# Graph network kernel: each step of finishing a block follows the step it needs by a group of sums, and the ring of gather places keeps its size up to the layers' ends

## The chip, the cores and the metric

The kernel runs on one core of one Trainium2 chip. The time is the device time of one execution in microseconds (us); smaller is better. The five engines named here are TensorE (PE; its weight loads are listed apart as PEld), VectorE (DVE), ScalarE (ACT), GpSimd (POOL) and SyncE (SP). Each works through its own list of instructions in order, and they wait for each other by semaphores. POOL and SP also issue DMA transfers.

## The reference

A graph with N = 6250 nodes of D = 512 features and E = 100000 edges, sorted by their destination. All is float32. The part that matters:

```python
h = relu(layernorm(x))
norm = -dinv[src] * dinv[dst]            # dinv = 1/sqrt(number of edges that leave a node)

def conv(h, W0, W1, b):
    gathered = segment_sum(h[src] * norm[:, None], dst, num_segments=N)
    return h @ W0 + gathered @ W1 + b

h = conv(h, W1_0, W1_1, b1)
h = leaky_relu(layernorm(h) * gamma + beta, 0.01)
return x + conv(h, W2_0, W2_1, b2)
```

So there are two layers, and each of them needs, for every node, the sum over its incoming edges of the rows of the source nodes, one product of that sum with a 512 x 512 matrix, and one product of the node's own row with another.

## The kernel before

**Edges, chunks and groups.** The edges are laid out in 782 chunks of at most 128 edges. Three chunks (STEP) belong to one window of 32 destination nodes, and four windows make a group, so a group has 12 chunks; there are 66 groups (NS) in a layer, of which the first has one window. The main loop runs over the layers and, in each, over the groups g.

**Gathers.** For each chunk POOL issues one indirect DMA (`gather_to`, L548), which fetches the 128 source rows of the chunk from a table in HBM into one of the numbered places of an array in SBUF (`places`). The function `ring` gives each chunk its place, and with it `prev`, the chunk that had that place before. At group g, `gather_to` issues every chunk whose place was last held by a chunk of a group that is already written into the program as summed; on the chip, POOL then waits for the sums of that earlier chunk. The ring has a size of 63 places in its first round and 55 in the next ones, and then shrinks round by round, to 35 (WIDE) in layer 0 and to 26 (NARROW) in layer 1.

**Sums.** DVE builds a one-hot matrix `sel` of edges against the 32 nodes of a window (`choose`, L689, from node numbers prepared by L678), one group ahead. In layer 0 DVE also multiplies it by the scale of the source rows, which came with the gathered rows (`scale`, L729). PE multiplies each of the group's 12 chunks with its part of `sel` into `ps` (`sums`, L745; 24 matmuls in the trace). ACT copies the result to SBUF as `agg` (L760). `sel` has three buffers, `ps` two, `agg` three.

**Finishing a block.** The nodes are also cut into 49 blocks of 128. Windows of 32 nodes drift against them, so a block takes its rows from two or three groups. For a block there are these steps on PE, with the others between:

1. *placing* (`place`, L781): PE multiplies the `agg` of the block's groups with one-hot matrices `there` (DVE, L768) into `an_ps`; ACT scales that to `an` (L880).
2. *transposes* (`first_half`, L888): four transposes of `an` into `hT_ps`; DVE copies them to `aT` (L890; one buffer).
3. *own products* (`own_products`, L648): the block's own rows, which SP loaded and DVE transposed to `hT` (L632), times the first matrix, into `u_ps` (two buffers).
4. *second products* (`second`, L643): `aT` times the second matrix, added into the same `u_ps`.
5. *finish*: in layer 0 DVE adds the bias and normalizes (L849 to L859), ACT and DVE apply the leaky relu (L862, L863), and SP stores the rows as the table of layer 1; in layer 1 DVE adds bias and x (L843, L844) and SP stores the output.

Three blocks are finished in four groups. `turn` does the loads, the DVE transposition of the own rows and the placing of one block; `second` of the block before is written in it ahead of the placing.

**What sets the order.** The lists of PE, POOL and SP are exactly in the order in which the program is written (`manual_schedule`). DVE and ACT are put in order by a scheduler, which follows the program with some freedom; `issue_after` forces single instructions behind others (so `scale` behind the last `there`, `aT` and the like, held in `behind`). In one pass of the group loop the program writes: the gathers; placing of the blocks that became complete, with the `second` of the block before; `sel` and `scale`; the group's sums; and then the transposes and own products of the blocks just placed. In groups 3 to 5 of layer 0 (SOON) the sums come first. From group 54 on (JOIN) a block's `second` follows its `first_half` directly (`dense`), and four of the last blocks (EARLY) have their own products made in advance.

## Time and profile before

| | |
|---|---|
| median of 3 runs | 2356.39 us (2353.88 to 2360.64) |
| the profiled execution | 2366.06 us |
| its span (first to last instruction) | 2364.3 us |
| mean granted clock of PE | 0.845 |
| PE matmuls busy | 1715.6 us (73% of the span) |
| POOL busy | 1490.9 us (63%) |
| DVE busy | 741.3 us (31%) |
| ACT busy | 332.3 us (14%) |

The profile is of one execution, whose span starts with the first instruction. A row of the timeline gives the start, the duration, the engine and line, what the instruction writes and reads with its shapes, how many equal instructions were drawn together (x), and in brackets how long the engine had been idle before and what ended that. The view of waits gives for an engine and line what it waited for, the total in us, how many times, and the longest. "issue" means a wait for nothing that the profile shows, "remote" that the releaser could not be named. The end of a PE matmul is modelled, so a PE row may end later in truth than the row says. The main loop of layer 0 fills the span to about 1250 us, that of layer 1 the rest.

### The profile page before, as it was taken

The page shows a single profiled execution, that of the slowest core. Times are in us where ns is not written, and L with a number is a line of the kernel's source. Part 1 is how long each engine was busy: PE and PEld are TensorE (multiplying, and loading weights), DVE is VectorE, ACT ScalarE, POOL GpSimd, SP SyncE. Part 2 cuts the span into 40 slices and gives each one's busy share as a digit, 9 for nine tenths or more (in the row PEclk, how much of TensorE's full clock was granted, in tenths as well). Part 3 has the DMA queues.
Part 4 walks back from the last instruction along what each step waited for, and adds up shares of the span by engine and source line. Part 5 has one row for each costly group of instructions (what it writes and reads, how often), then busy time and mean ns, then how long its engine had stood idle before and what let it go on. Part 6 is the DMA issues. An engine that isn't in the chain of part 4 may idle for free.

```text
span 2364.3 us, 18838 instructions
## 1 busy us (share of the span) xinstructions
PE 1715.6 (73%) x6458; PEld 663.8 (28%) x6458; DVE 741.3 (31%) x1554; ACT 332.3 (14%) x605; POOL 1490.9 (63%) x1578
## 2 busy tenths in 40 slices
PE   5377876676788767777757577787767787676777
PEld 4233322222233222222222222222222222222223
DVE  8754433323334334332323112221112122112221
ACT  8564110101011110110100000000000000000000
POOL 4545566666676666666645666666666666666663
PEclk9668987888888888888877788887888888888888
DMA  9976777777787767777756777777777776777773
GB/s 352 348 239 194 202 217 209 214 214 209 214 238 205 209 198 219 217 219 206 227 151 178 209 231 222 215 216 216 215 223 213 227 219 202 223 231 223 228 214 117
DMA packets 225517, 515.56 MB, mean 218 GB/s; under 512 B 38795, under 2 KB 90569, under 8 KB 225413
## 3 DMA queue, kind: packets, MB, share of 16 engines
q0 software_dynamic: 125120, 415.88, 59.9%
q1 hardware_dynamic: 100253, 98.38, 13.2%
q8 instruction: 53, 0.87, 0.2%
q14 instruction: 51, 0.42, 0.1%
q10 hardware_dynamic: 40, 0.02, 0.0%
HBM read 475.25 MB, written 38.86 MB: 217 GB/s over the span
## 4 chain that ended last, share of the span: by engine, by line
PE 40%; another core or an unknown queue 25%; issue 15%; POOL 9%; DVE 6%; DMA 2%; ACT 2%; SPq 0%; DVEq 0%; ACTq 0%; POOLq 0%
PE u_ps L643 12%; PE ps L745 9%; POOL places L548 9%; PE u_ps L648 9%; PE an_ps L781 6%; PE hT_ps L888 2%; DMA places<-tab,sidx 1%; DVE hi L417 1%; DVE aT L890 1%; DVE lo L417 1%; ACT agg L760 1%; DVE sel L689 1%; DVE there L768 1%; PE hT_ps L598 1%
## 5 line engine op out<-in xcount | busy, mean ns | idle before, releaser
L548 POOL DMA_INDIRECT places<-tab,sidx x1191 | 1133.1, 951 | 604.6 <-issue 332.9
L745 PE MATMUL ps<-places,sel 128*32 128x512 f32 x3104 | 461.2, 656 | 56.9 <-issue 50.8
L781 PE MATMUL an_ps<-agg,there 128*128 128x512 f32 (+1 forms) x554 | 281.1, 635 | 109.7 <-ACT agg L760 65.0
L548 POOL DMA_INDIRECT places<-tab,lidx x270 | 256.2, 949 | 129.2 <-issue 74.1
L643 PE MATMUL u_ps<-places,aT 128*128 128x512 f32 x384 | 226.0, 742 | 140.4 <-DVE aT L890 136.6
L689 DVE TENSOR_TENSOR sel<-dlx,nodes_ps 128x384 f32<-128x384 f32 (+3 forms) x134 | 72.4, 541 | 723.3 <-remote 518.9
L643 PE MATMUL u_ps<-w,aT 128*128 128x512 f32 x384 | 208.1, 692 | 83.2 <-DVE aT L890 71.0
L745 PEld LDWEIGHTS ps<-places,sel 128*32 128x32 f32 x3104 | 101.3, 117 | 391.3 <-issue 367.1
L760 ACT ACTIVATE agg<-ps 128x512 f32<-128x512 f32 (+2 forms) x130 | 76.4, 590 | 938.5 <-remote 667.1
L648 PE MATMUL u_ps<-w,hT 128*128 128x512 f32 x392 | 198.5, 647 | 9.7 <-issue 9.6
L648 PE MATMUL u_ps<-places,hT 128*128 128x512 f32 x392 | 189.9, 625 | 9.8 <-issue 9.7
L781 PEld LDWEIGHTS an_ps<-agg,there 128*128 128x128 f32 (+1 forms) x554 | 104.1, 197 | 261.0 <-issue 183.6
L643 PEld LDWEIGHTS u_ps<-places,aT 128*128 128x128 f32 x384 | 88.7, 241 | 276.5 <-DVE aT L890 165.7
L888 PE MATMUL hT_ps<-ident,an 128*128 128x128 f32 x384 | 69.8, 309 | 117.5 <-ACT an L880 67.5
L643 PEld LDWEIGHTS u_ps<-w,aT 128*128 128x128 f32 x384 | 82.8, 222 | 204.5 <-issue 115.6
L768 DVE TENSOR_SCALAR there<-iota_r,node_of 128x128 f32<-128x128 f32 (+1 forms) x286 | 66.9, 294 | 154.1 <-remote 71.6
L632 DVE STREAM_TRANSPOSE hT<-h 128x512 f32<-128x512 f32 x90 | 63.5, 705 | 139.5 <-PE u_ps L648 44.9
L648 PEld LDWEIGHTS u_ps<-w,hT 128*128 128x128 f32 x392 | 78.2, 210 | 96.9 <-issue 96.1
L888 PEld LDWEIGHTS hT_ps<-ident,an 128*128 128x128 f32 x384 | 44.6, 152 | 206.2 <-issue 120.6
L648 PEld LDWEIGHTS u_ps<-places,hT 128*128 128x128 f32 x392 | 75.2, 202 | 89.3 <-issue 89.3
L843 DVE SCALAR_TENSOR_TENSOR u_ps<-u_ps,root,bias 128x512 f32<-128x512 f32 x45 | 34.1, 759 | 202.5 <-PE u_ps L643 105.2
L849 DVE TENSOR_TENSOR u_ps<-u_ps,bias 128x512 f32<-128x512 f32 x45 | 31.5, 699 | 183.4 <-PE u_ps L643 66.0
(196 smaller groups left out, 1139.2 us busy)
## 6 DMA issues: line engine op xcount, KB each, us to landing
h<-tab SPq DMA_DIRECT2D x360, 64.0 KB
places<-tab,sidx POOLq DMA_INDIRECT x1191
xt<-in_x_dram SPq DMA_DIRECT2D x48, 256.0 KB
out_dram<-t SPq DMA_DIRECT2D x48, 256.0 KB
tab<-t SPq DMA_DIRECT2D x46, 256.0 KB
tab<-places SPq DMA_DIRECT2D x22, 528.0 KB
places<-in_x_dram SPq DMA_DIRECT2D x5, 1792.0 KB
places<-tab,lidx POOLq DMA_INDIRECT x270
```

What stands on the lines that cost most here:

```text
L417: made = nc.vector.tensor_tensor(t, s[:, g * 2 * GJ : (g + 1) * 2 * GJ].rearrange("p (j s) -> p j s", s=2)[:, :, None, :] .to_broadcast([E ...
L548: nc.gpsimd.indirect_dma_start(out=places[:, slot(t), :] if own_scale else zr(layer, t), out_offset=None, in_=x if layer == 0 and t < RAW ...
L632: nc.vector.transpose(hT.rearrange("p k (a i) -> p k a i", i=Q), own_h.pop(i).rearrange("p (a k d) -> p k a d", a=NQ, d=Q))
L643: nc.tensor.matmul(u_ps[:r], hT[:, kc, :r], w[:, kc, :], start=(start and kc == 0), stop=(stop and kc == KD - 1))
L648: nc.tensor.matmul(u_ps, hT[:, kc, :], w[:, kc, :], start=(kc == 0), stop=(stop and kc == KD - 1))
L689: nc.vector.tensor_tensor(sel[:, q : q + k, :w, :], of, node[:, q : q + k, None, :].to_broadcast([P, k, w, Q]), op=OP.is_equal)
L745: members.append(nc.tensor.matmul(to, sel[:, q, s, :], rows_of, start=(s == 0), stop=(s == len(chunk[q]) - 1 and (cnt is None or chunk[q][ ...
L760: nc.scalar.activation(agg[g][: n * Q, lo : lo + w], ps[: n * Q, lo : lo + w], AF.Copy)
L768: behind[1] = nc.vector.tensor_scalar(t[:m, :r], iota_r[:m, :r], node_of[:m, g : g + 1], -(1.0 + i * P), op0=OP.subtract, op1=OP.is_equal)
L781: all_of.append(nc.tensor.matmul(placed[i][:r], t[:m, :r], agg[g][:m, :], start=(g == inside[i][0]), stop=(g == inside[i][-1])))
L843: nc.vector.scalar_tensor_tensor(v, v, root[:r, i : i + 1], bias2[:r], op0=OP.mult, op1=OP.add)
L888: nc.tensor.transpose(ps[:, kc, :r], an[:r, kc * P : (kc + 1) * P], ident[:r, :r])
```

## The change

In groups 0 to 47 of both layers (`deep`; DEEP = 18 groups are left then) the steps are written in another order. A pass of the loop now holds: the gathers, `sel` of the next group and (layer 0) `scale` of the next group; the sums of the group; `second` of the block whose transposes were written in an earlier pass; the transposes and own products of the blocks placed in an earlier pass; and then the placing of the blocks that are complete now. At group 48 what is outstanding is written out at once. From group 48 to 53 the placing stands ahead of the sums, as before, and `second` of the block before comes behind the sums instead of ahead of the placing; from group 54 on only the ring is different. The special case of groups 3 to 5 is gone. The extra buffers for `agg` (`wide`, every other group, in buffers named `pre`) are used up to group 47 in both layers instead of up to group 7 of layer 0. The ring keeps 55 places until 165 chunks or fewer are left in a layer, and then shrinks by 8 (DROP) a round to 35 or 26; in layer 1 it goes back to 55 first. The numbers of instructions are the same but for two fewer on DVE.

The diff:

```diff
@@ -38,6 +38,8 @@
 SPREAD = 16
 WIDE = 35
 NARROW = 26
+DROP = 8
+DEEP = 18
 
 
 def parts(r):
@@ -54,10 +56,9 @@
             prev.append(last.get(k, -1))
             last[k] = len(slots)
             slots.append(k)
-        if size == most:
-            size = full
-        elif len(slots) > most + 2 * full:
-            size -= 2 if size > WIDE else 3 if size > NARROW and len(slots) > chunks + full else 0
+        layer, at = divmod(len(slots), chunks)
+        left = chunks - at
+        size = full if left > 3 * full else max(WIDE if layer == 0 else NARROW, size - DROP)
     return slots[: 2 * chunks], prev[: 2 * chunks]
 
 
@@ -497,7 +498,6 @@
                           "minus unsorted dinv sdinv bias1 bias2 gam bet unseen unit N E D NB NC NU NS KD rows places "
                           "R load_rest sc pick quads src_hi zero_row p_id lent X src W").split())
     AHEAD = 2
-    SOON = range(3, 6)
     EARLY = {NB - 4: NS - 13, NB - 3: NS - 11, NB - 2: NS - 9, NB - 1: NS - 7}
     ACT = mybir.EngineType.Activation
     UN = STEP * P * N / E
@@ -753,7 +753,7 @@
                                                         late[NB - LATE + b][:r], start=False, stop=(b == LATE - 1)))
             if closes:
                 together(f"sums{layer}_{g}", members)
-                wide = layer == 0 and g < SOON.stop + 2 and g % 2
+                wide = 3 * layer <= g < NS - DEEP and g % 2
                 agg[g] = pool.tile([P, D], F32, name="pre" if wide else "agg", bufs=3)
                 w = D // 2 if g == NS - 1 else D
                 for lo in range(0, D, w):
@@ -865,7 +865,7 @@
             for lo, hi in parts(r):
                 nc.sync.dma_start(tab[1][at + lo : at + hi, :], t[lo:hi])
 
-        def turn(layer, i, left=()):
+        def turn(layer, i):
 
             r = rows[i]
             if layer == 1 and i not in EARLY:
@@ -873,8 +873,6 @@
             if i + AHEAD < NB:
                 load(layer, i + AHEAD)
             hT = None if i in EARLY else own(layer, i)
-            for k, aT in left:
-                second(layer, k, aT)
             place(layer, i, [g for g in inside[i] if i < NB - 1 or g == NS - 1])
             an = pool.tile([P, D], F32, name="an")
             nc.scalar.activation(an[:r], placed.pop(i)[:r], AF.Copy,
@@ -960,7 +958,7 @@
             nc.vector.tensor_reduce(ok, wrong[:, :n], AX.X, OP.add)
             nc.vector.tensor_single_scalar(unseen, ok, 0.0, op=OP.is_gt)
 
-        checking = check()
+        checking, scaled = check(), None
 
         find("ps")
         find("ps")
@@ -973,7 +971,7 @@
                 gathered = AHEAD_OF
                 for i in range(AHEAD):
                     load(layer, i)
-            i, chosen, left = 0, {}, []
+            i, chosen, left, due = 0, {}, [], []
             for g in range(NS - 1):
                 gather_to(layer, STEP * unit[g])
                 if layer == 0 and g == NS // 2:
@@ -984,36 +982,42 @@
                     look_up("hT_ps")
                     find("hT_ps")
                     assert looked >= min(RAW, STEP * unit[g + 1])
-                due = []
+                deep = g < NS - DEEP
 
                 def finished():
-                    at_i, rest = i, left
-                    if g == NS - JOIN or inside[at_i].stop > g:
-                        for k, aT in rest:
-                            second(layer, k, aT)
-                        rest = []
+                    at_i = i
                     while inside[at_i].stop <= g:
-                        due.append((at_i, turn(layer, at_i, rest)))
-                        rest = []
+                        due.append((at_i, turn(layer, at_i)))
                         at_i += 1
-                    return at_i, []
-
-                soon = layer == 0 and g in SOON
-                if not soon:
-                    i, left = finished()
+                    return at_i
+
+                if g == NS - DEEP:
+                    for k, aT in left:
+                        second(layer, k, aT)
+                    left = [(k, first_half(layer, k, hT, an)) for k, (hT, an) in due]
+                    due = []
+                if not deep:
+                    rest, left, due = left, [], []
+                    i = finished()
                 if g == NS - 2 and layer == 0:
                     assert i >= NB - LATE and gathered == NC
                     gather_ahead(STEP * unit[g])
                 sel, chunk = chosen.pop(g) if g in chosen else choose(g)
-                if layer == 0:
+
+                def scale_for(some):
                     with ExitStack() as order:
                         for ins in behind.values():
                             order.enter_context(tc.issue_after(ins.ins))
-                        scaled = scale(sel, chunk)
+                        return scale(*some) or scaled
+
+                if layer == 0 and not 0 < g <= NS - DEEP:
+                    scaled = scale_for((sel, chunk))
                 with ExitStack() as order:
                     if layer == 1 and g == 0:
                         order.enter_context(tc.issue_after(behind_rows[0].ins))
                     chosen[g + 1] = choose(g + 1)
+                if layer == 0 and deep:
+                    scaled = scale_for(chosen[g + 1])
                 cnt = None
                 if layer == 1:
                     with ExitStack() as order:
@@ -1022,10 +1026,14 @@
                         cnt = count_late(sel, chunk)
                 if g < NS - 2:
                     sums(layer, g, sel, chunk, cnt)
-                    if soon:
-                        i, left = finished()
+                    for k, aT in left if deep else rest:
+                        second(layer, k, aT)
+                    if deep:
+                        left = [(k, first_half(layer, k, hT, an)) for k, (hT, an) in due]
+                        due = []
+                        i = finished()
                 else:
-                    assert len(due) == 1 and due[0][0] == NB - 3 and all(len(c) == STEP for c in chunk)
+                    assert not rest and len(due) == 1 and due[0][0] == NB - 3 and all(len(c) == STEP for c in chunk)
                     if layer:
                         half = [[(s, q) for s in range(STEP) for q in range(at, at + NQ // 2)] for at in (0, NQ // 2)]
                         step = [half[0][:-2], half[0][-2:], half[1]]
@@ -1056,7 +1064,7 @@
                     find("hT_ps")
                 if g < NS - JOIN - 1 and inside[i].stop <= g + 1:
                     theres[i] = spots(i, inside[i])
-                for k, (hT, an) in due:
+                for k, (hT, an) in due if not deep else ():
                     if g < NS - JOIN:
                         left.append((k, first_half(layer, k, hT, an)))
                     else:
```

The list of PE in layer 1, some 30 groups in, before. `ps` are a group's sums, `an_ps` a placing, `hT_ps` the transposes, `u_ps` own and second products; the numbers are buffers, equal numbers belong together:

```order
L745 MATMUL ps_7629<-places_94,sel_7577 32x512 x12
L781 MATMUL an_ps_7671<-agg_7521,there_7644 128x512
L781 MATMUL an_ps_7671<-agg_7592,there_7645 128x512
L781 MATMUL an_ps_7671<-agg_7642,there_7646 128x512
L745 MATMUL ps_7680<-places_94,sel_7627 32x512 x12
L888 MATMUL hT_ps_7701<-ident_62,an_7675 128x128 x4
L648 MATMUL u_ps_7708<-places_94,hT_7669 128x512 x4
L643 MATMUL u_ps_7708<-places_94,aT_7706 128x512 x4
L781 MATMUL an_ps_7742<-agg_7592,there_7695 128x512
```

The same engine and place after (lines below 886 have moved by up to two):

```order
L745 MATMUL ps_7742<-places_94,sel_7681 32x512 x12
L886 MATMUL hT_ps_7757<-ident_62,an_7719 128x128 x4
L648 MATMUL u_ps_7764<-places_94,hT_7713 128x512 x4
L781 MATMUL an_ps_7778<-agg_7575,there_7721 128x512
L781 MATMUL an_ps_7778<-pre_7640,there_7722 128x512
L781 MATMUL an_ps_7778<-agg_7696,there_7723 128x512
L745 MATMUL ps_7805<-places_94,sel_7740 32x512 x12
L643 MATMUL u_ps_7764<-places_94,aT_7762 128x512 x4
```

The second products (L643) of a block stood right behind its own products (L648); now the next block's placing and a group of sums stand between them.

The list of DVE in the middle of layer 0, before. The first row builds `sel` of a later group, L890 copies the transposes, L729 is the scale, L632 transposes the block's own rows, and L849 is the first step of the finish:

```order
L689 TENSOR_TENSOR sel_3386<-dlx_73,nodes_ps_98 128x384
L890 COPY aT_3272<-hT_ps_3267 128x512
L729 TENSOR_TENSOR sel_3244<-sel_3244,places_94 128x352
L729 TENSOR_TENSOR sel_3244<-sel_3244,places_94 128x32
L678 TENSOR_TENSOR nodes_ps_98<-nodes_ps_98,iota_r_63 128x128
L632 STREAM_TRANSPOSE hT_3296<-h_3148 128x512
L849 TENSOR_TENSOR u_ps_3274<-u_ps_3274,bias1_78 128x512
```

The same after (the copy of the transposes is now L888):

```order
L689 TENSOR_TENSOR sel_2931<-dlx_73,nodes_ps_98 128x384
L678 TENSOR_TENSOR nodes_ps_98<-nodes_ps_98,iota_r_63 128x128
L849 TENSOR_TENSOR u_ps_2763<-u_ps_2763,bias1_78 128x512
L888 COPY aT_2836<-hT_ps_2831 128x512
L852 BN_STATS st_2817<-u_ps_2763 128x6
L729 TENSOR_TENSOR sel_2862<-sel_2862,places_94 128x384
L853 BN_AGGR mv_2818<-st_2817 128x2
```

The first step of a block's finish (L849) has moved ahead of the next block's copy of transposes, and the scale stands amid the finish; the scale there belongs to the group after the one whose sums PE does next.

## The prediction

> **What bounds the kernel now.** I read the stretches by engine first, then the waits, then one piece of the timeline. The windows of POOL's gather line, over layer 0 from group 8 to 62 and layer 1 from group 6 to 62, give duration, POOL busy time and count, PE's clock, DMA share and GB/s:
>
> ```profile
> 266.60:1166.70 900.10, 597.87 (x628) 0.86 0.75 215
> 1354.00:2304.00 950.00, 628.68 (x663) 0.85 0.73 220
> ```
>
> The waits of POOL in the same two stretches (us in total, times, longest), layer 0 first:
>
> ```profile
> POOL places L548 <- issue: 174.3, 570, 0.8
> POOL places L548 <- remote: 75.4, 26, 4.6
> POOL places L548 <- PE ps L745: 21.4, 5, 6.2
> POOL places L548 <- PE u_ps L648: 16.3, 6, 3.5
> POOL places L548 <- PE hT_ps L888: 12.3, 5, 2.7
> ...
> POOL places L548 <- issue: 186.0, 598, 4.0
> POOL places L548 <- remote: 84.4, 31, 4.6
> POOL places L548 <- PE u_ps L648: 25.1, 9, 4.5
> POOL places L548 <- PE hT_ps L888: 13.9, 5, 3.9
> POOL places L548 <- PE ps L745: 5.5, 1, 5.5
> ```
>
> A gather takes 597.87/628 = 0.952 us, and 174.3/570 = 0.306 us of issue lies ahead of it: 1.26 us, 15.1 us for a group of 12. Everything beyond that is pauses. In layer 0 there are 26 + 5 + 6 + 5 = 42 pauses, 125.4 us; in layer 1 31 + 9 + 5 + 1 = 46, 128.9 us. With 0.306 us of issue taken off each, 112.5 and 114.8 us can be lost, over 54 and 56 groups: **2.07 us a group**, 1.29 and 1.22 groups a pause. DMA at 0.75 and 0.73 is not full. So the cadence is POOL's: a stream of gathers, then a pause until places are freed by finished sums. The question is what ends a pause. PE, layer 1:
>
> ```profile
> 1704.13 1.12 PE L888 MATMUL hT_ps<-ident,an 128*128 128x128 f32 x4
> 1705.04 3.89 PE L648 MATMUL u_ps<-places,hT 128*128 128x512 f32 x8
> 1708.76 3.60 PE L643 MATMUL u_ps<-places,aT 128*128 128x512 f32 x8
> 1712.20 2.74 PE L781 MATMUL an_ps<-agg,there 128*128 128x512 f32 x6
> 1714.87 2.78 PE L745 MATMUL ps<-places,sel 128*32 128x512 f32 x24
> 1717.58 0.66 PE L888 MATMUL hT_ps<-ident,an 128*128 128x128 f32 x4
> 1718.07 3.60 PE L648 MATMUL u_ps<-places,hT 128*128 128x512 f32 x8
> 1722.79 3.70 PE L643 MATMUL u_ps<-places,aT 128*128 128x512 f32 x8 [1.11 <-DVE aT L890]
> 1726.42 2.78 PE L745 MATMUL ps<-places,sel 128*32 128x512 f32 x24
> 1729.13 1.98 PE L781 MATMUL an_ps<-agg,there 128*128 128x512 f32 x4
> 1737.99 2.08 PE L781 MATMUL an_ps<-agg,there 128*128 128x512 f32 x2 [6.88 <-ACT agg L760]
> ```
>
> POOL and ACT at the same place:
>
> ```profile
> 1704.47 0.95 POOL L548 DMA_INDIRECT places<-tab,sidx  x1 [5.46 <-PE ps L745]
> ...
> 1718.26 0.95 POOL L548 DMA_INDIRECT places<-tab,sidx  x1 [0.31 <-issue]
> 1721.81 0.95 POOL L548 DMA_INDIRECT places<-tab,sidx  x1 [2.60 <-PE u_ps L648]
> ...
> 1735.60 0.95 POOL L548 DMA_INDIRECT places<-tab,sidx  x1 [0.31 <-issue]
> 1737.52 0.95 POOL L548 DMA_INDIRECT places<-tab,sidx  x1 [0.96 <-remote]
> ...
> 1714.97 0.69 ACT L880 ACTIVATE an<-an_ps,ndeg 128x512 f32<-128x512 f32 x1 [10.08 <-issue]
> 1721.57 0.60 ACT L760 ACTIVATE agg<-ps 128x512 f32<-128x512 f32 x1 [5.91 <-remote]
> 1737.34 0.60 ACT L760 ACTIVATE agg<-ps 128x512 f32<-128x512 f32 x1 [15.17 <-remote]
> ```
>
> The sums of 1714.87 end by their records at 1717.65, yet ACT's copy of them starts at 1721.57, 3.9 us later with ACT idle; POOL resumes at 1721.81. The next sums end at 1729.20 and are copied at 1737.34, 8.1 us later; POOL resumes at 1737.52. Both times the release comes 0.8 to 2.4 us after the last gather of the stream ended (1719.21, 1736.55). But the placing that ends at 1714.94 is answered at 1714.97, and the transposes of 1704.13 let L643 start at 1708.76 without a wait, while those of 1717.58 hold it to 1722.79. A row of PE counts its matmuls; each has a weight load beside it. From the stream's start at 1704.47, the prompt placing ends about 16 + 16 + 12 = 44 PE instructions in; the late sums end at 44 + 48 = 92. In the next stream, from 1721.81, the late sums end at 16 + 48 = 64. **I read this as a hold: within a stream of gathers, what PE finishes in its first 50 or so instructions is signalled at once, the rest only when the stream pauses.**
>
> [...]
>
> **The change part by part.** PE's waits over the whole span, with ACT's for the sums:
>
> ```profile
> PE u_ps L643 <- DVE aT L890: 207.7, 48, 14.8
> PE hT_ps L888 <- ACT an L880: 67.5, 11, 13.5
> PE an_ps L781 <- ACT agg L760: 65.0, 14, 6.9
> ...
> ACT agg L760 <- remote: 667.1, 65, 27.7
> ```
>
> *Order on PE, groups 0 to 47 of each layer.* From transposes to the products that need them there stand 16 instructions now (L648), and 16 + 12 + 48 = 76 or more after; from placing to transposes 48 now, 48 or 64 after; from sums to placing 24 to 40 now, about 140 after. So the 207.7 + 67.5 + 65.0 = 340 us of PE waiting mostly go. None of it is a direct gain, since POOL has the longer period: PE's rows of a group at full clock are 2.78 + 0.75 × (0.66 + 3.60 + 3.60 + 2.74) = 10.7 us against 15.1. It gains only if the sums are signalled earlier. Needed are 48 + 0.75 × (8 + 16 + 16 + 12) = 87 PE instructions a group. If PE no longer stops at a fixed step, the end of the first sums in a stream falls evenly into 87 instructions; it is within the first 56 (between the prompt 44 and the late 64) with chance 0.64. Then POOL gets its next 12 places in time and the stream is 24 long; the second sums, 87 further, are held. That is 1.64 groups a pause, where now it is 1.22 to 1.29. A longer stream has a longer pause, as these two of 21 rows behind streams of 24 show (first and last):
>
> ```profile
> 317.92 0.95 POOL L548 DMA_INDIRECT places<-tab,sidx  x1 [4.02 <-remote]
> ...
> 2304.53 0.94 POOL L548 DMA_INDIRECT places<-tab,lidx  x1 [4.46 <-remote]
> ```
>
> So 3.9 us after a long stream (4.24 less 0.306) and 2.3 after a short one (the 2.60 above): 0.64 × 3.9 + 0.36 × 2.3 = 3.3 us per 1.64 groups, 2.03 a group: a gain of 0.04 × 82 groups = 3 us (40 in layer 0 from group 8, 42 in layer 1 from group 6). Were every pause 2.3, it would be 1.40 a group and 55 us. Behind the waits removed, PE will have less left to do when a stream ends, since it did not stand at L643, and the long pauses' extra 1.6 us is such rest; so I take a value between, nearer the lower: **24 us**.
>
> [...]
>
> *Scale ahead of its group (DVE L729, layer 0).* DVE now waits for the gathers of group g+1 with the transposes' copy and the block's finish queued behind it. POOL is up to 55 places ahead, 4.6 groups, so they have landed: 0. If that cover were gone, each group would wait out one gather batch, 15.1 us less the 10.7 of PE's work: 4.4 × 40 = 176 us slower; nothing speaks for it.
>
> *Ring of 55 instead of falling to 35 and 26.* Layer 0 runs at 900.1/628 = 1.433 us a gather with a ring of 63 to 35, layer 1 at 950/663 = 1.433 with 35 to 26. The ring's size shows no effect: 0, between −20 gathers × (1.433 − 1.26) = −3.5 us and +3.5, when the lead is given back in the last rounds.
>
> *Flush at group 48, later groups, SOON, wide buffers, SP.* One step is issued back to back once a layer; POOL's lead of 4.6 groups covers it: 0, or twice PE's longest wait, 29.6 us, if not. In groups 48 to 53 the products follow the sums too; 12 groups at the same rate, 3 us, within my rounding. SP's loads of x and h are issued one step before their use as before: 0.
>
> *Sum.* 24 us off the profiled execution's 2366.1 us (span 2364.3 and 1.8 around it) is 2342; the median of the runs is 9.7 us under that execution, so 2356.4 − 24 = **2332 us**.
>
> **Rivals.** *PE's waiting was the bound.* If the sums really last until their signal, each removed wait is time gained until POOL runs without pauses: 2.07 × 82 = 170 us, 2186 us. For it: the chain of PE's waits is 340 us. Against: the prompt placing, and ACT's 667.1 us of waiting with PE idle in the same pieces.
>
> *Nothing changes.* The waits removed end with the pause anyway (L643 at 1722.79, POOL at 1721.81); PE then stands at the next step. If sums still fall late in the stream, a pause still frees 1.2 to 1.3 groups, and the ring is never used: 2356, within 7 us.
>
> *Slower: longer streams, longer holds.* With 55 places POOL may go on for 24 to 36 gathers while PE's signals, DVE's copies and ACT's agg all wait for the end of it. If every pause is then as long as the longest ordinary one above, 4.6 us (4.3 without issue), at 1.64 groups each, that is 2.62 a group, 0.55 × 82 = 45 us: 2401. It decides once the mean pause passes 1.64 × 2.07 = 3.4 us; my own 3.3 for it lies just under that, which is why it weighs.
>
> **How the numbers follow.** Runs of this kernel spread from 2353.88 to 2360.64, so 0.3%, 7 us, is what a measurement can tell. Likeliest (−3 to −55): 0.47, of which 0.05 lies within 7 us. PE the bound: 0.10. Nothing: 0.13. Slower: 0.30. Faster 0.47 − 0.05 + 0.10 = 0.52; same 0.13 + 0.05 = 0.18; slower 0.30. The range takes the likeliest, nothing and the slower case up to 2400, and below some way into the first rival: 2275 to 2400; the likeliest alone gives 2301 to 2353.
>
> **What would show it.** Right: PE's waits for aT, an and agg fall from 340 us to under 120; POOL's pauses in a stretch fall from 42 to some 33, more of them behind streams of 24; ACT still waits for sums well after their records' end. In layer 1, L643 stands right behind L745 with no wait. Wrong: PE's waits gone and pauses as many as before (nothing), means over 3.4 us (slower), or POOL busy above 70% of a stretch, now 66% (PE the bound). Also wrong if DVE shows long waits at L729.

## The result

The kernel after takes 2379.5 us (median of 20 runs, 2362.6 to 2398.5), the kernel before 2360.0 us beside it (20 runs, 2352.9 to 2369.8): a ratio of 1.0077, 95% interval 1.0058 to 1.0096, so 0.8% **slower**, clear of the noise. The forecast was 2332 us. The profiled execution of after has a span of 2381.6 us, 17.3 us more than that of before. One thing is needed to read the numbers below: in some visits (runs made together on one chip) both kernels take some 330 to 350 us less than in others (before: 2033 or 2360 us), so each run is compared with the runs of before in its own visit, and the two kinds are kept apart.

The windows of POOL's gather line in the kernel after, over the two stretches that the prediction used for before:

```profile
266.60:1166.70 900.10, 587.18 (x615) 0.85 0.75 212
1354.00:2304.00 950.00, 618.29 (x653) 0.83 0.73 217
```

Before, these were x628 and x663: 13 and 10 gathers are missing, some 14 to 19 us. POOL's waits there, layer 0 first:

```profile
POOL places L548 <- issue: 171.9, 563, 0.5
POOL places L548 <- remote: 45.8, 14, 4.6
POOL places L548 <- PE ps L745: 44.3, 8, 9.7
POOL places L548 <- PE an_ps L781: 19.1, 7, 4.3
POOL places L548 <- PE u_ps L643: 14.8, 4, 4.3
POOL places L548 <- PE u_ps L648: 6.8, 2, 4.3
POOL places L548 <- PE hT_ps L886: 6.4, 3, 2.3
...
POOL places L548 <- issue: 185.0, 606, 0.6
POOL places L548 <- remote: 77.1, 20, 9.2
POOL places L548 <- PE ps L745: 29.5, 6, 7.8
POOL places L548 <- PE hT_ps L886: 10.7, 3, 4.6
POOL places L548 <- PE u_ps L648: 10.1, 4, 4.4
POOL places L548 <- PE an_ps L781: 9.2, 6, 2.6
POOL places L548 <- PE u_ps L643: 8.6, 2, 4.6
```

The pauses are fewer (14 + 8 + 7 + 4 + 2 + 3 = 38 instead of 42, and 41 instead of 46) and longer; together they are 137.2 and 145.2 us, where they were 125.4 and 128.9. ACT's waits for the sums and PE's waits, over the whole span:

```profile
ACT agg L760 <- remote: 320.4, 31, 27.7
...
ACT pre L760 <- remote: 154.8, 15, 37.9
...
PE u_ps L643 <- issue: 117.5, 102, 3.2
PE hT_ps L886 <- issue: 98.9, 33, 13.5
PE ps L745 <- issue: 92.3, 98, 2.8
...
PE u_ps L643 <- DVE aT L888: 24.4, 6, 6.2
```

PE's waits for `aT`, 207.7 us before, are down to 24.4. In their place stand waits on "issue", nothing that the profile names, in many short pieces. The timeline of PE shows what they look like; the stream of gathers, whose next one is the POOL row below, runs there from 1367.40 to 1397.21:

```profile
1377.01 2.78 PE L745 MATMUL ps<-places,sel 128*32 128x512 f32 x24
1380.96 0.66 PE L886 MATMUL hT_ps<-ident,an 128*128 128x128 f32 x4 [1.17 <-ACT an L878]
1381.46 2.31 PE L648 MATMUL u_ps<-places,hT 128*128 128x512 f32 x5
1384.41 0.59 PE L648 MATMUL u_ps<-places,hT 128*128 128x512 f32 x1 [0.64 <-issue]
1385.81 0.59 PE L648 MATMUL u_ps<-places,hT 128*128 128x512 f32 x1 [0.81 <-issue]
1387.21 0.59 PE L648 MATMUL u_ps<-places,hT 128*128 128x512 f32 x1 [0.81 <-issue]
1388.61 0.59 PE L781 MATMUL an_ps<-agg,there 128*128 128x512 f32 x1 [0.81 <-issue]
1390.02 1.01 PE L781 MATMUL an_ps<-agg,there 128*128 128x512 f32 x1 [0.82 <-issue]
...
1399.81 1.01 PE L745 MATMUL ps<-places,sel 128*32 128x512 f32 x1 [0.39 <-issue]
...
1401.63 0.95 POOL L548 DMA_INDIRECT places<-tab,sidx  x1 [4.42 <-remote]
```

Where nothing stops PE it now runs ahead, and from 1384.41 on its matmuls mostly start 1.40 us apart (each with its weight load, so 0.70 us an instruction). These steps last until 1401.21, 4 us past the stream's end, and POOL goes on at 1401.63. From 1367.40 to 1384.41 it started at least 16 (L643) + 12 (L781) + 48 (L745) + 8 (L886) + 10 (L648) = 94 instructions; if 0.70 us each holds from the stream's start, 24 of them were finished in these 17 us, which leaves about 70 outstanding. This is an estimate, for no row shows when an instruction was finished, and what sets that number was not shown.

At the start of layer 1, POOL and ACT in the kernel after:

```profile
1288.40 0.95 POOL L548 DMA_INDIRECT places<-tab,sidx  x1 [2.21 <-PE ps L745]
...
1357.27 0.95 POOL L548 DMA_INDIRECT places<-tab,sidx  x1 [0.30 <-issue]
1367.40 0.95 POOL L548 DMA_INDIRECT places<-tab,sidx  x1 [9.19 <-remote]
...
1298.46 0.60 ACT L760 ACTIVATE agg<-ps 128x512 f32<-128x512 f32 x1 [5.65 <-remote]
...
1367.17 0.60 ACT L760 ACTIVATE pre<-ps 128x512 f32<-128x512 f32 x1 [37.94 <-remote]
```

The ring has grown back to 55 places, so POOL issues 56 gathers in one stream of 70 us, and ACT copies no sums between 1298.46 and 1367.17. From there on the sums of layer 1 are late, while the gathers are not. The difference of after to before in us, for the same gather and the same group's copy of sums, counted from the start of the span in both traces (gathers are numbered over all indirect DMAs of POOL; neighbours differ by a few us):

| in the program | layer 0, early | layer 0, middle | end of layer 0 | layer 1, early | layer 1, middle | layer 1, late |
|---|---|---|---|---|---|---|
| gather no. | 160: −14.1 | 560: −13.4 | 760: +3.1 | 880: −6.6 | 1200: +2.4 | 1480: +10.5 |
| copy of sums no. | 8: −15.0 | 44: −0.3 | 64: +1.4 | 72: +32.1 | 104: +47.7 | 132: +17.3 |

So 14 us are gained in the first groups, lost again at the end of layer 0; and in layer 1 the sums fall 32 to 48 us behind, of which 17 us are left when the layer ends. 29 more places (55 instead of 26) at 1.433 us a gather are 41.6 us.

### The profile page after: what moved, and what is told of

Read it like the earlier page. It is cut to its first block, busy times and chain, and to the rows that moved or that the text cites. A ratio compares the mean times of both kernels' runs of the same rounds, so it can differ in the third digit from the quotient of the medians.

```text
span 2381.6 us, 18793 instructions
## 1 busy us (share of the span) xinstructions
PE 1771.9 (74%) x6458; PEld 677.4 (28%) x6458; DVE 734.5 (31%) x1551; ACT 332.6 (14%) x605; POOL 1495.5 (63%) x1578
## 4 chain that ended last, share of the span: by engine, by line
PE 55%; issue 18%; another core or an unknown queue 10%; POOL 8%; DVE 6%; DMA 2%; ACT 1%; DVEq 0%; POOLq 0%; SPq 0%; ACTq 0%
PE u_ps L643 15%; PE ps L745 15%; PE u_ps L648 13%; PE an_ps L781 8%; POOL places L548 7%; PE hT_ps L886 2%; DMA places<-tab,sidx 2%; DVE hi L418 1%; DVE lo L418 1%; PE hT_ps L598 1%; DMA src_c<-in_src_dram 0%; DVE st L852 0%; PE both_ps L441 0%; DMA places<-tab,lidx 0%
## 5 line engine op out<-in xcount | busy, mean ns | idle before, releaser
L745 PE MATMUL ps<-places,sel 128*32 128x512 f32 x3104 | 508.4, 643 | 103.3 <-issue 92.3
L643 PE MATMUL u_ps<-w,aT 128*128 128x512 f32 x384 | 217.5, 692 | 69.3 <-issue 57.8
L643 PE MATMUL u_ps<-places,aT 128*128 128x512 f32 x384 | 214.6, 687 | 73.1 <-issue 59.8
L745 PEld LDWEIGHTS ps<-places,sel 128*32 128x32 f32 x3104 | 110.6, 115 | 455.0 <-issue 404.1
L648 PE MATMUL u_ps<-places,hT 128*128 128x512 f32 x392 | 203.6, 654 | 31.7 <-issue 29.8
L648 PE MATMUL u_ps<-w,hT 128*128 128x512 f32 x392 | 197.4, 643 | 16.7 <-issue 15.8
L781 PE MATMUL an_ps<-agg,there 128*128 128x512 f32 (+1 forms) x340 | 180.5, 631 | 28.0 <-issue 18.5
L886 PE MATMUL hT_ps<-ident,an 128*128 128x128 f32 x384 | 73.6, 314 | 136.3 <-issue 98.9
L760 ACT ACTIVATE agg<-ps 128x512 f32<-128x512 f32 (+2 forms) x87 | 50.8, 586 | 643.9 <-remote 320.4
L643 PEld LDWEIGHTS u_ps<-places,aT 128*128 128x128 f32 x384 | 78.4, 213 | 211.0 <-issue 186.0
L643 PEld LDWEIGHTS u_ps<-w,aT 128*128 128x128 f32 x384 | 78.9, 214 | 206.4 <-issue 186.2
L781 PE MATMUL an_ps<-pre,there 128*128 128x512 f32 x232 | 125.6, 622 | 6.5 <-issue 6.5
L632 DVE STREAM_TRANSPOSE hT<-h 128x512 f32<-128x512 f32 x90 | 63.6, 707 | 210.1 <-remote 70.0
L648 PEld LDWEIGHTS u_ps<-places,hT 128*128 128x128 f32 x392 | 79.1, 211 | 123.7 <-issue 123.7
L886 PEld LDWEIGHTS hT_ps<-ident,an 128*128 128x128 f32 x384 | 51.0, 158 | 217.9 <-issue 167.4
L648 PEld LDWEIGHTS u_ps<-w,hT 128*128 128x128 f32 x392 | 78.2, 210 | 104.1 <-issue 102.4
L781 PEld LDWEIGHTS an_ps<-agg,there 128*128 128x128 f32 (+1 forms) x340 | 66.6, 199 | 123.7 <-issue 112.4
L888 DVE COPY aT<-hT_ps 128x512 f32<-128x512 f32 x96 | 65.9, 686 | 106.6 <-remote 61.8
```

The source lines that it names most:

```text
L632: nc.vector.transpose(hT.rearrange("p k (a i) -> p k a i", i=Q), own_h.pop(i).rearrange("p (a k d) -> p k a d", a=NQ, d=Q))
L643: nc.tensor.matmul(u_ps[:r], hT[:, kc, :r], w[:, kc, :], start=(start and kc == 0), stop=(stop and kc == KD - 1))
L648: nc.tensor.matmul(u_ps, hT[:, kc, :], w[:, kc, :], start=(kc == 0), stop=(stop and kc == KD - 1))
L745: members.append(nc.tensor.matmul(to, sel[:, q, s, :], rows_of, start=(s == 0), stop=(s == len(chunk[q]) - 1 and (cnt is None or chunk[q][ ...
L760: nc.scalar.activation(agg[g][: n * Q, lo : lo + w], ps[: n * Q, lo : lo + w], AF.Copy)
L781: all_of.append(nc.tensor.matmul(placed[i][:r], t[:m, :r], agg[g][:m, :], start=(g == inside[i][0]), stop=(g == inside[i][-1])))
```

## The experiments

Two questions had to be told apart: which part of the change costs the time, and what makes the pauses on which the whole forecast rested.

**Ring alone, order alone, ring of one layer.** Before with the new `ring` (the new constant DROP is left out here):

```diff
-        if size == most:
-            size = full
-        elif len(slots) > most + 2 * full:
-            size -= 2 if size > WIDE else 3 if size > NARROW and len(slots) > chunks + full else 0
+        layer, at = divmod(len(slots), chunks)
+        left = chunks - at
+        size = full if left > 3 * full else max(WIDE if layer == 0 else NARROW, size - DROP)
```

> The order of the kernel before, with the ring of the kernel after (55 places up to the layers' ends). Theory R (the ring costs): gathers keep their pace, since pauses grow with the streams, and a larger ring only makes the sums later against the gathers, which the end of layer 1 must make up; in the kernel after the sums of layer 1 were 41 to 47 us later at the same group and 17 us of it were left at the end. Expected then: 10 to 20 us slower than before, sums of layer 1 some 40 us later in the middle. Theory O (the order costs: each block is finished a group later, and that latency is paid at the layers' ends): within 5 us of before.

After with the old one (the diff the other way round):

> The order of the kernel after, with the ring of the kernel before (63, 55, then down to 35 and 26). Theory R: within 5 us of before, or a little faster, with PE's waits for aT gone and POOL's pauses per gather as before. Theory O: 10 to 20 us slower, as the kernel after. My forecast on record (the order gives 24 us, the ring 0) would have it 24 us faster.

After with the new ring in layer 0 only; layer 1 goes down by 8 a round to 26:

```diff
-        size = full if left > 3 * full else max(WIDE if layer == 0 else NARROW, size - DROP)
+        size = (full if left > 3 * full else max(WIDE, size - DROP)) if layer == 0 else max(NARROW, size - DROP)
```

> The kernel after, but in layer 1 the ring goes straight down to 26 places (8 a round) instead of back to 55; layer 0 keeps 55 to its end. Theory R: layer 0 of the kernel after ended only 1.4 us later than before, so the time is within 5 us of before, 15 us faster than the kernel after. Theory O: as the kernel after, 15 to 20 us slower than before.

And in layer 1 only, with layer 0 as before:

```diff
-        size = full if left > 3 * full else max(WIDE if layer == 0 else NARROW, size - DROP)
+        if layer == 0:
+            if size == most:
+                size = full
+            elif len(slots) > most + 2 * full:
+                size -= 2 if size > WIDE else 0
+        else:
+            size = full if left > 3 * full else max(NARROW, size - DROP)
```

> The kernel after, but in layer 0 with the ring of before (down to 35 two by two); only layer 1 keeps 55 places to its end. On a chip with pauses, theory R (each layer's ring costs what its end cannot make up): with layer 0's ring alone costing 0.43% and both 0.8%, 0.2 to 0.6% slower than before; if only layer 0's ring costs, within 0.2% of before. On a chip without pauses: 6 to 10 us faster than before, as the order alone.

Measured, as ratios to before of the same visit with 95% intervals, all in visits with pauses: ring alone **1.0063** (1.0039 to 1.0087), order alone **1.0009** (0.9979 to 1.0039), new order with the ring of layer 0 1.0043 (1.0024 to 1.0062), with that of layer 1 1.0059 (1.0034 to 1.0084). Theory O falls: the order alone is not slower, and the ring alone has nearly all of the loss. Theory R holds in the main, with one miss: for the ring of layer 0 it said within 5 us of before, and 8 us more were measured (2369.6 against 2361.5). That share is just clear of the order alone in the same visit (0.33%, 0.01 to 0.65%); the share of layer 1 is surer. The windows of the gather line over 130 to 266, 640 to 1160 and 2100 to 2310 us, of before:

```profile
130.00:266.00 136.00, 63.63 (x67) 0.85 0.70 199
640.00:1160.00 520.00, 342.38 (x360) 0.87 0.75 215
2100.00:2310.00 210.00, 139.46 (x148) 0.86 0.75 223
```

of after:

```profile
130.00:266.00 136.00, 75.57 (x79) 0.85 0.77 215
640.00:1160.00 520.00, 337.32 (x352) 0.87 0.75 212
2100.00:2310.00 210.00, 132.82 (x141) 0.92 0.76 225
```

of the order alone:

```profile
130.00:266.00 136.00, 75.76 (x80) 0.83 0.79 217
640.00:1160.00 520.00, 341.87 (x358) 0.87 0.76 215
2100.00:2310.00 210.00, 138.88 (x147) 0.88 0.75 223
```

of the ring alone:

```profile
130.00:266.00 136.00, 64.78 (x69) 0.86 0.71 201
640.00:1160.00 520.00, 332.07 (x349) 0.86 0.73 208
2100.00:2310.00 210.00, 138.44 (x147) 0.93 0.78 229
```

and, of the new order with the new ring in layer 1 only, the last of these stretches:

```profile
2100.00:2310.00 210.00, 128.63 (x136) 0.89 0.73 215
```

The order brings POOL 12 or 13 gathers further in the first groups of layer 0 (79 and 80 against 67), and no more after that. The ring takes 8 to 11 gathers from the end of layer 0 (352 and 349 against 360). At the end of layer 1 the kernel after loses 7 (141 against 148), and the one with the new order and the ring in layer 1 loses 12 (136). The ring alone did not lose there; its sums of layer 1 were 38 to 50 us late in the middle and 14 us at the end, of which 11 came from layer 0, so in one profile its layer 1 made nearly all of it up. One profile can't settle such shares: the order alone and the new order with the new ring in layer 1 only have the same layer 0, and at its end their copies of sums are 4.6 and 15.9 us ahead of before, 11 us apart. Of PE's waits, the ring alone has 353.7 us for `aT` (207.7 before), so what the order removes is a wait that costs nothing: with it, the ring costs 0.6%, and without it as well.

**What makes the pauses: PE's instructions?** First, three quarters of own and second products left out (run few_products, 69 PE instructions a group instead of 87), then also two of three chunks of the sums (37 instructions; few_sums, made three times, the last one called few_sums_c):

```diff
-            for kc in some:
+            for kc in (some if start or len(some) < KD else (KD - 1,)):
...
-            for kc in range(KD):
-                nc.tensor.matmul(u_ps, hT[:, kc, :], w[:, kc, :], start=(kc == 0), stop=(stop and kc == KD - 1))
+            for kc in range(1):
+                nc.tensor.matmul(u_ps, hT[:, kc, :], w[:, kc, :], start=True, stop=stop)
...
-            for s, q in some:
+            for s, q in [k for k in some if k[0] == 0 or n < NQ or not 1 < g < NS - 2]:
...
```

> The kernel before with fewer instructions on PE: of the four parts of the own products and of the second products of a block only one each is computed (the rest of the product is left out, except in blocks whose own products are made in advance), so 69 PE instructions a group instead of 87. Theory H (pauses are set by how many PE instructions are outstanding): streams of 24 become more frequent than 21 of 90, and pauses fall, but by less than half. Theory P (PE itself is the bound, 17.1 us for 87 instructions): 69 need 13.6 us, less than POOL's 15.1, so pauses nearly vanish and the time falls by 150 us or more. Theory G (the gathers have a pace of 1.43 us of their own, whatever PE does): the pace in the middle of both layers stays within 1% of 1.433 us a gather.

> The kernel before with most of PE's work left out: one of the four parts of own and second products, and of the sums only the first of three chunks of each window, in all groups but the first two and the last two (37 PE instructions a group instead of 87). The gathers are the same. Theory H: all that a stream of 12 needs is then within PE's first 56 instructions, pauses vanish, pace 1.25 us a gather, 200 us faster. Theory D: the pace stays within 2% of 1.43 us in both layers.

> The kernel before with 37 PE instructions a group instead of 87 (of own and second products one part of four, of the sums the first chunk of three in each window; the rest is left out). On a chip with pauses: theory H (they come from PE's instructions outstanding) says pauses vanish, 1.25 us a gather, 200 us faster; theory D (the gathers' own pace) says 1.43 us a gather as before. On a chip without pauses: as in the last run, 10 us faster than before.

> The kernel before with 37 PE instructions a group instead of 87 (one part of four of own and second products, the first chunk of three of each window in the sums; the rest is left out), a third time, because both runs before fell on chips without pauses. On a chip with pauses: theory H says pauses vanish, 200 us faster than before; theory D says 1.43 us a gather as before. On a chip without: 10 us faster.

few_products took 2348.5 us against 2361.5 in its visit. Theory P, which wanted 150 us, falls by that; the paces, 733.4/502 = 1.46 and 500/353 = 1.42 us, miss the 1% of theory G narrowly, and longer streams were what theory H had said too. few_sums fell twice on visits without pauses (2022.0 against 2033.4, 2020.2 against 2033.2) and once on one with: 2335.3 against 2360.5. The windows of the gather line in that run, and after them those of before:

```profile
266.60:1000.00 733.40, 488.25 (x512) 0.69 0.76 215
1400.00:1900.00 500.00, 335.73 (x354) 0.68 0.74 222
...
266.60:1000.00 733.40, 484.88 (x510) 0.85 0.75 213
1400.00:1900.00 500.00, 330.44 (x350) 0.84 0.73 218
```

With less than half of PE's instructions the gathers keep their pace, 1.43 and 1.41 us against 1.44 and 1.43. The run gains 25 us and not 200; theory H falls as it stood. PE's steps of 1.40 us are gone as well (matmuls that start 1.35 to 1.45 us after the one before: 1 here, 18 before, 117 in after), and the pauses stay. Streams only become longer: 36 gathers and then 5.5 us of pause, in the mean of eleven in layer 1, where before has 2.5 us after 12 (mean of 55) and 4.35 us after 24 (mean of 22). Twelve gathers more lengthen stream and pause together by 12 × 1.254 + 1.84 = 16.9 us there, 1.41 us a gather, which is near the 1.40 us of PE's steps; that the two are one thing was not shown. Over all runs with pauses, the idle time between streams (gaps over 1 us from 260 us on, without the one between the layers) is 245 to 298 us, least with 51 pauses in few_sums_c; before has 273 us in 90.

**Or the bytes?** Layer 1 gathers rows of half the size, from wrong addresses:

```diff
-                    out=places[:, slot(t), :] if own_scale else zr(layer, t), out_offset=None,
-                    in_=x if layer == 0 and t < RAW else tab[layer],
+                    out=places[:, slot(t), :] if own_scale else zr(layer, t)[:, : D // 2] if layer else zr(layer, t), out_offset=None,
+                    in_=x if layer == 0 and t < RAW else tab[1].rearrange("n (a d) -> (n a) d", a=2) if layer else tab[0],
```

> The kernel before, but in layer 1 each gather fetches rows of 1 KB instead of 2 KB, from wrong addresses (the sums of layer 1 are then wrong; nothing else is left out). Theory D (the pace of 1.43 us a gather is that of the transfer itself, 256 KB each, and the pauses are the time in which it catches up): pauses of layer 1 vanish, pace 1.25 us, layer 1 shorter by 100 us or more. Theory H (the pauses come from PE's late signals): the pace of layer 1 stays within 2% of 1.43 us and pauses after streams of 12 stay at 2 us.

> The kernel before, but each gather of layer 1 fetches rows of 1 KB instead of 2 KB, from wrong addresses (nothing else is left out). In the runs with pauses, the last packet of a stream's gathers ends 2.2 to 2.9 us after the stream whether it had 12, 24 or 36 gathers, but the pause grows: 2.4, 4.3, 6.0 us. Theory S (the completion signals of the gathers, as many for each gather whatever its bytes, are worked off more slowly than POOL issues gathers, and PE's signals wait behind them): on a chip with pauses, pace of layer 1 stays at 1.43 us, time within 15 us of before. Theory D (the bytes): 1.25 us in layer 1, 100 us faster. On a chip without pauses: within 5 us of before.

> The kernel before with rows of 1 KB in layer 1's gathers instead of 2 KB (from wrong addresses; nothing else left out), a third time, because the first two fell on chips without pauses. On a chip with pauses: theory S (completion signals) says pace of layer 1 at 1.43 us a gather and time within 15 us of before; theory D (bytes) says 1.25 us and 100 us faster.

Two of the three fell on visits without pauses (2033.1 against 2033.4, 2030.8 against 2035.3). The third took 2393.9 us against 2382.3. Its windows of the gather line:

```profile
266.60:1000.00 733.40, 479.92 (x506) 0.83 0.74 211
1400.00:1900.00 500.00, 328.40 (x349) 0.81 0.43 127
```

The DMA share falls from 0.73 to 0.43 and the pace stays at 500/349 = 1.43 us: theory D falls. From the packets, the last one of a stream ends some 1.6 us after it in layer 1 of that run and 2.2 to 3.0 us in the others, after 12 gathers as after 24; the pauses there are 2.7 and 4.4 us. What is left is a price for each gather, 0.17 us beside POOL's own 1.26, which stays when its bytes are halved and nearly stays when PE's instructions are cut to less than half. That it is the gathers' completion signals (theory S) was not shown.

**A pause put in by hand.** A copy of one column on POOL after every 12th gather of layer 1 (the tile `pause` is new):

```diff
+                if layer == 1 and t % 12 == 5 and 60 < t < NC - 24:
+                    nc.gpsimd.tensor_copy(pause, zr(layer, t)[:, :1])
```

> The kernel before, with one small POOL instruction (a copy of one column of the gathered rows) after every 12th gather of layer 1, in the middle of a group's gathers, so that POOL waits there until that gather has landed, some 2.3 us each, about 58 times. Theory S: on a chip with pauses PE's signals pass in these pauses, POOL finds its places free at the next group, and the old pauses shrink by about as much: layer 1 within 40 us of before. If the old pauses came from PE's own work (theory H), they stay, and the 58 new ones add 130 us. On a chip without pauses: 110 to 150 us slower.

> The kernel before with a small POOL instruction after every 12th gather of layer 1, which waits for that gather to land, once more; where gathers run without pauses it added 224 us. Where they pause: theory S (what holds PE's signals is a backlog that grows by some 0.15 us with each gather and is worked off in any pause) says that the new pauses take the place of the old ones, layer 1 grows by less than 60 us and the whole is under 2430 us. Theory H (the old pauses are PE's own need of time) says the old ones stay and the new ones add 130 us or more: over 2490 us.

Both fell on visits without pauses: 2259.5 against 2035.3 and 2256.9 against 2032.8, 224 us more for 58 waits, 3.9 us each, where 110 to 150 us were expected. The question that they were made for, whether such waits take the place of the pauses, stays open.

**Without pauses.** After and the order alone, in one visit:

> The kernel after once more, to see whether its loss belongs to the pauses. On the chip of the last three runs the kernel before takes 2033 us, POOL streams without pauses and ACT copies the sums 0.14 us (median) after their records' end, where it was 5.2 us on the chip of the runs before that. If this runs on a chip without pauses: theory R (the ring's cost comes with the pauses, which make the sums late by the ring's length) says within 5 us of before; theory E (the cost is paid at the layers' ends whatever the pace, since the shrinking ring holds gathers back there) says 10 to 20 us slower. If it runs on a chip with pauses: 0.6 to 1.0% slower than before, as measured.

> The order of the kernel after with the ring of before, once more. Without pauses: 3 to 8 us faster than before, since layer 0 of the last runs' kernel with this order and this ring in layer 0 was 6 us ahead of the unchanged order at the end of layer 0. With pauses: within 0.4% of before, as measured.

After took 2025.4 us against 2033.2, **0.9965** (0.9951 to 0.9979), the order alone 2025.2, 0.9964 (0.9950 to 0.9977). The windows of the gather line in after, and its waits in 1400 to 1900 us (POOL) and over the span (ACT):

```profile
266.60:1000.00 733.40, 553.54 (x584) 0.90 0.86 246
1400.00:1900.00 500.00, 378.14 (x401) 0.94 0.85 255
...
POOL places L548 <- issue: 117.9, 387, 0.3
...
ACT agg L760 <- PE ps L745: 428.5, 68, 15.5
```

Here a gather takes 1.256 and 1.247 us, POOL waits for hardly anything but issue, and ACT's releaser is named: the sums. The order gains 8 us, and the larger ring is free (2025.4 against 2025.2); theory R had put after within 5 us of before, and the order's gain takes it beyond that. Theory E (the ends cost whatever the pace) falls.

**Shorter rings.** With the order of after, first the ring of before but down to 17 places in layer 1 (NARROW = 18), then a ring that goes straight down to 35 and 22, whose diff to after is:

```diff
-NARROW = 26
+NARROW = 22
...
-        left = chunks - at
-        size = full if left > 3 * full else max(WIDE if layer == 0 else NARROW, size - DROP)
+        size = max(WIDE if layer == 0 else NARROW, size - DROP)
```

> The order of the kernel after with the ring of the kernel before, except that in layer 1 the ring falls to 17 places instead of 26. Theory R (a larger ring only makes the sums later, which the end of the layer must make up; the gathers keep their pace of 1.43 us): sums of layer 1 some 9 x 1.43 = 13 us earlier in the middle, and the time 3 to 8 us under the kernel with 26 places, so 0.1 to 0.4% faster than before. If instead places run out for PE's next group, the pauses grow and it is slower by more than 10 us.

> The order of the kernel after with a ring that falls at once, by 8 a round, to 35 places in layer 0 and 22 in layer 1. Theory R with S: on a chip with pauses the sums follow the gathers by the ring's length, so those of layer 1 come 4 x 1.43 = 6 us earlier than with 26, and layer 0 has less to make up at its end: 3 to 12 us faster than before. On a chip without pauses the ring matters only if it starves PE (17 places did): 3 to 8 us faster than before, as the order alone, unless 22 starve it too.

> The order of the kernel after with the ring falling at once to 35 and 22 places, once more; on a chip without pauses it took 0.9969 of before. On a chip with pauses, theory R says the sums of layer 1 come 6 us earlier against the gathers than with 26 places, and the time is 3 to 12 us under before.

17 places, in a visit without pauses, are too few: 1.0072 (1.0054 to 1.0091); a gather in the middle of layer 1 takes 500/386 = 1.30 us there. What 17 places do in a visit with pauses was not measured. The ring down to 35 and 22 took 0.9969 (0.9955 to 0.9984) of before without pauses and 0.9983 (0.9958 to 1.0009) with them, 4 us of the 3 to 12 expected, and not clear of no change. So the order with a short ring beats before where POOL does not pause, and is not clearly different where it does; it and the order alone are the best of what was tried over both kinds, and no run tells the two apart.

## Why the prediction was wrong, point by point

*What bounds the kernel* (POOL's gathers and the pauses behind them): right. *What sets the pauses* (a hold by PE's outstanding instructions): wrong as the cause. PE does run into something like such a hold, and the kernel after shows it in steps of 1.40 us, but with PE's instructions cut to less than half the steps are gone and 245 of 273 us of pauses are left, where none were to be. What the gathers cost beyond POOL's own time goes with their number, so a stream of 24 is followed by a pause nearly twice as long as a stream of 12 (4.35 against 2.5 us). What makes that cost stays open.

*The order, 24 us, taken between 3 and 55.* This is the step that failed first. Its own formula at the measured pauses gave 3 us, and in the middle of the layers the pauses came out so: fewer, longer, and the gathers no faster (508 in 266.60 to 1000 us against 510, and 350 in 1400 to 1900 us in both). The choice of 24 rested on the sentence that the extra 1.6 us of a long pause is work that PE would no longer have left. With 37 instructions left of 87 the pauses behind 36 gathers are still 5.5 us. Measured for the order alone: 0.1% slower, interval 0.2% faster to 0.4% slower. What the order does gain, 12 gathers or 14 us in the first groups of layer 0, the prediction did not see, nor that most of it is lost again by the end.

*The ring, 0 within 3.5 us.* This is the step that gave the result its sign: 0.6%, 15 us for the ring alone. Pace by ring size was read rightly (1.433 us in both layers), but the conclusion that the size has no price was not. In the visits with pauses POOL stops only when its places run out (in before it goes on at 1721.81 and 1737.52, 0.24 and 0.18 us after a copy of sums starts), and the sums follow the gathers by a whole ring. A larger ring therefore does not bring the gathers forward, it puts the sums back, by 29 × 1.433 = 41.6 us in layer 1 (measured 32 to 48). At the layer's end that has to be made up, and some of it isn't. The price belonged to the last groups of each layer, and the sum was made from the middle.

*Scale, flush, wide buffers, SP at 0:* no run speaks against it; the order alone holds them all, but none was run by itself. The long waits of DVE at L729 that would have spoken against it did not come (1.4 us in after).

*The rivals.* "PE's waiting was the bound" did not come about: those waits went and nothing was gained. "Nothing changes" is what the order did. "Slower" had the right sign and a chance of 0.30, by another mechanism: mean pauses did rise (137.2/38 = 3.6 us, 3.3 without issue, just under the 3.4 from which this rival counted), but over more gathers each; the loss came from the ring. That 2379.5 us lies within the stated range is luck: the range reached up to 2400 for this rival, and not for the ring. Of the signs named, these were right: PE's waits for `aT`, `an` and `agg` (24.4 + 36.0 + 5.9 = 66 us, under 120 as said), L643 behind L745 without a named wait, and ACT's late sums. Fewer pauses (38 for 42, where 33 was said) were right in direction, at less than half the size; more of them stand behind streams of 24, as said (35 against 22 over the run).

*PE as the bound.* That case would have given 170 us; the runs with fewer PE instructions, 13 and 25 us faster where there are pauses, decide against it. When the matmuls themselves end was not shown, for the ends of PE's records are modelled; ACT's copy of the sums started 0.14 us (median) after these ends here without pauses and some 5 us with them.

## What to carry to other kernels

When a producer stops only because its buffers are full, the consumer runs a whole ring behind it, and a larger ring buys delay, not pace (here 29 more places put the sums of layer 1 back by 32 to 48 us, with 350 gathers in 1400 to 1900 us before and after; where POOL did not stop, the larger ring was free, 2025.4 against 2025.2 us): price it at the ends of the loop, where the delay has to be worked off. Removing a wait gains nothing while another engine has the longer period (here PE's waits for `aT` fell from 207.7 to 24.3 us with the order alone, at a ratio of 1.0009); ask which engine's period it shortens before taking a value above the lower bound. Cut the suspected cause to a fraction in one run before building a sum on it: here a kernel with 37 of 87 instructions would have spoiled the mechanism of the forecast.

## What the runs showed of the hardware

The same kernel took 2033 us in some visits to a chip and 2360 to 2382 us in others, and the chip with number 3 appeared with both. In the visits with 2360 to 2382 us, gathers have a pace of 1.43 us instead of 1.25, the sums' copies start some 5 us (median) after the records' end instead of 0.14, and PE's matmuls, where it runs ahead in a stream of gathers, mostly start 1.40 us apart (117 steps of 1.35 to 1.45 us in after, 18 in before). The extra cost goes with the number of gathers, not with bytes (0.43 of DMA share instead of 0.73, 1.43 us a gather in both) and hardly with the number of PE's instructions (37 a group instead of 87, 1.41 and 1.43 us). The granted clock of PE is lower in them too (0.84 to 0.85 against 0.91 in the medians of before), but a lower clock alone was not a longer time: with 37 instructions a group it was 0.70, and that run took 2335.3 us against 2360.5 of before. What decides between the two kinds of visit was not found.
